# Two mixture-of-experts layers: fewer padded tiles, row copies on another engine, and a longer lead for the staged weights

## The chip, the cores and the metric

One Trainium2 chip, one core of it. The metric is the device time of one execution of the whole program in microseconds, and the number given for a kernel is the median of its timed runs. Lower is better.

## The reference, cut to what matters

The input is 8 sequences of 1024 tokens with 128 features in fp32, 8192 tokens in all. Two layers follow one another, each with an attention part and a mixture-of-experts part, each part added to its input:

```python
x = x + L0_attn(layernorm(x))      # softmax attention, 8 heads of 32, low-rank keys and values
x = x + L0_ffn(layernorm(x))       # 14 experts of width 256, each token goes to its best 2, GELU
x = x + L1_attn(layernorm(x))      # linear attention, 16 heads of 8
x = x + L1_ffn(layernorm(x))       # 8 experts of width 512, each token goes to its best 1, ReLU
```

The second expert part has a limit: an expert keeps at most `ceil(8192 / 8 * 1.25)` = 1280 tokens, those with the highest probability; a token that it turns away goes to expert 0. The first expert part has no limit.

## The kernel before, in words

The program has four stages one after the other: attention of layer 0 (up to about 1335 us), experts of layer 0 (to about 1505), attention and routing of layer 1 (to about 1915), experts of layer 1 (to the end).

**How experts are done.** While routing, the kernel scatters each token's row into a table in HBM (`rows_in` for layer 0, `rows1` for layer 1) that has a region for each expert. The expert stage then walks over tiles of 256 rows (`TW0`), each tile belonging to one expert. How many tiles an expert needs is known only on the chip: its token count over 256, rounded up. `expert_tables` (L147) computes it. `upto` is the running sum of tiles over the experts; `exp_j` (L173) holds the expert of each tile and `row_j` (L188) the first row of each tile. The number of tiles in the program is fixed: `NT0` = 64 + 14 = 78 for layer 0 (L34) and `NT1` = 32 + 8 = 40 for layer 1 (L59). A tile beyond those in use reads a spare region of padding rows; in layer 1 its rows carry a destination that is out of range and are not written.

`looked_up` (L191, load at L198) brings the table entries into registers, six tiles at a time: row numbers to SyncE's registers, expert numbers to VectorE's.

**A tile of layer 0** (L885 to L933), function by function:

- `fetch`: SyncE issues a DMA of 256 rows into `xr` (L888), six buffers.
- `stage`: VectorE copies the weights of the tile's expert from the resident `blob` into `wt` (L896), three buffers. The expert's number comes from a register.
- `turn`: TensorE transposes the rows into `px` (L902), and VectorE copies that from PSUM to `xt` (L904).
- `hidden0`: TensorE multiplies by the first weights into `ph` (L911), and ScalarE applies GELU into `g` (L914).
- `output0`: TensorE multiplies by the second weights into `py` (L921, two buffers), VectorE adds bias (L926) and row (L930) into `y`, and GpSimd issues the DMA to `rows_out` (L931).

The loop (L941 to L956) is software-pipelined and its order is written out by hand for TensorE, VectorE and SyncE (`manual_schedule`, L935). Round j fetches tile j+4, stages and turns tile j+1, does the first product of tile j and the second product of tile j-1. ScalarE and GpSimd are ordered by the scheduler.

**Places.** After the loop in the source, but outside the part with the fixed order, L963 to L970 work out where each token's two results lie in `rows_out`: for each of 8 sequences and 2 choices, four small VectorE operations (compare, multiply, reduce, subtract) give `found`. The scheduler puts these 64 operations early: in the profile they run from 1321.8 to 1347.5 us, among the table computations and the first tiles. The gathers of layer 1 (L1052) read `found`.

**A tile of layer 1** (L1509 to L1564) is the same with a hidden width of 512, so four products into `ph` (L1536), ReLU on ScalarE (L1539), and eight products into `py` (L1546). Its result is scattered straight to the output by two indirect DMAs from GpSimd (L1558). After the 40 tiles every engine loads the number `over`, the largest token count of experts 1 to 7 (L1504), and branches (L1588): if it is over 1280, `dropped` (L1596) finds the tokens that are turned away by bisection and sends them through expert 0, in 16 blocks of 512 tokens.

The order of a round in layer 0's loop, before the change:

```python
if j + 4 < NT0:
    ahead.append(fetch(j + 4))
if ahead:
    t = ahead.pop(0)
    ready.append((t, stage(j + 1), turn(t)))
t, w, xt = ready.pop(0)
made.append((j, t, w, hidden0(w, xt)))
if len(made) > 1:
    output0(*made.pop(0))
```

Of the kernel before, what the change touches and what calls it, by code (L numbers as in the profile page):

```python
# [8 lines left out]
F32 = mybir.dt.float32  # L9
# [19 lines left out]
E0, F0 = 14, 256  # L29
K0 = F0 // P  # L30
CAP0 = NB * T
TW0 = 256
TI0 = TW0 // P
NT0 = 2 * NB * T // TW0 + E0  # L34
REG0 = TW0 + CAP0
ROWS0 = E0 * REG0 + TW0

# [1 line left out]
B_END = B_B2 + D  # L39
# [8 lines left out]
E1, F1 = 8, 512  # L48
# [7 lines left out]
NBLK = NB * T // BLK  # L56


NT1 = NB * T // TW0 + E1  # L59
ROWS1 = E1 * REG0 + TW0  # L60
RW1 = 2 * D + 1
L_W1, L_W2, L_B1, L_B2 = 0, F1, F1 + K1 * D, F1 + K1 * D + K1
# [13 lines left out]
def tile_two_layers(  # L76
# [70 lines left out]
    def expert_tables(tab, psum, ptag, counts, ne, nt):  # L147

        tot = psum.tile([P, ne], F32, name="tot", tag=ptag)
        nc.tensor.matmul(tot, lhsT=ones, rhs=counts, start=True, stop=True)
        per = CAP0 // TW0
        grid = tab.tile([P, ne, per], F32, name="grid")
        nc.vector.tensor_tensor(
            grid, tot.unsqueeze(2).to_broadcast([P, ne, per]),
            cst[:, C_TW:C_TW + per].unsqueeze(1).to_broadcast([P, ne, per]), ALU.is_gt,
        )
        tiles = tab.tile([P, ne], F32, name="tiles")
        nc.vector.tensor_reduce(tiles, grid, AX.X, ALU.add)  # L160
# [27 lines left out]
        nc.vector.tensor_copy(row_j, rj)  # L188
        return SimpleNamespace(exp_j=exp_j, row_j=row_j, base=base, tot=tot)

    def looked_up(table, nt, engine, top):  # L191

# [681 lines left out]
    with ExitStack() as ph:  # L874
# [10 lines left out]
        def fetch(j):  # L885
            r = row_of(j)
            t = work.tile([P, TI0, D], F32, name="xr", bufs=6)
            nc.sync.dma_start(  # L888
                out=t, in_=rows_in[bass.ds(r, TW0), :].rearrange("(p i) d -> p i d", i=TI0)
            )  # L890
            return t

        def stage(j):
            e = expert_of(j)
            t = work.tile([P, 1, B_END], F32, name="wt", bufs=3)
            nc.vector.tensor_copy(t, blob[:, bass.ds(e, 1), :])  # L896
            return t[:, 0, :]

        def turn(t):
            ps = px.tile([P, TI0, P], F32, name="px")  # L900
            for i in range(TI0):
                nc.tensor.transpose(ps[:, i, :], t[:, i, :], ident)  # L902
            xt = work.tile([P, TW0], F32, name="xt", bufs=3)
            nc.vector.tensor_copy(xt, ps.rearrange("p i t -> p (i t)"))  # L904
            return xt

        def hidden0(w, xt):
# [9 lines left out]
        def output0(j, t, w, g):  # L917
# [14 lines left out]
                out=rows_out[j * TW0:(j + 1) * TW0, :].rearrange("(p i) d -> p i d", i=TI0), in_=y  # L932
            )  # L933

        with tc.manual_schedule(  # L935
            engines={mybir.EngineType.PE, mybir.EngineType.DVE, mybir.EngineType.SP}
        ):
            made, ahead = [], [fetch(j) for j in range(4)]
            t = ahead.pop(0)
            ready = [(t, stage(0), turn(t))]  # L940
            for j in range(NT0):  # L941
                if j + 4 < NT0:
                    ahead.append(fetch(j + 4))
                if ahead:
                    t = ahead.pop(0)
                    ready.append((t, stage(j + 1), turn(t)))
                t, w, xt = ready.pop(0)
                made.append((j, t, w, hidden0(w, xt)))
                if len(made) > 1:
                    output0(*made.pop(0))  # L950
                if j == 8:
                    load_layer1()
                    make_layer1()
                if j == NT0 - 8:
                    warm()
            output0(*made.pop(0))  # L956


        shape = [P, CPB, E0]
        for b in range(NB):  # L960
            for k in range(2):
                pick = work.tile(shape, F32, name="pick")
                nc.vector.tensor_tensor(  # L963
                    pick, chosen[:, k, b, :].unsqueeze(2).to_broadcast(shape),
                    cst[:, C_J:C_J + E0].unsqueeze(1).to_broadcast(shape), ALU.is_equal,
                )
                nc.vector.tensor_tensor(pick, pick, tables0.base.unsqueeze(1).to_broadcast(shape), ALU.mult)
                to = work.tile([P, CPB], F32, name="to")
                nc.vector.tensor_reduce(to, pick, AX.X, ALU.add)
                nc.vector.tensor_tensor(found[:, b, k, :], ranks[:, k, b, :], to, ALU.subtract)  # L970

    layer0w.close()


# [518 lines left out]
    with ExitStack() as ph:  # L1493
        tab = ph.enter_context(tc.tile_pool(name="d_tab", bufs=1))
        over = tab.tile([1, 1], mybir.dt.int32, name="over")
        with ExitStack() as main:
            work = main.enter_context(tc.tile_pool(name="d_work", bufs=2))
            px = main.enter_context(tc.tile_pool(name="d_px", bufs=2, space=PSUM))
            ph_ps = main.enter_context(tc.tile_pool(name="d_ph", bufs=4, space=PSUM))
            py_ps = main.enter_context(tc.tile_pool(name="d_py", bufs=2, space=PSUM))  # L1500

            tables = expert_tables(tab, px, "px", counts1, E1, NT1)
            most = tab.tile([1, 1], F32, name="most")
            nc.vector.tensor_reduce(most, tables.tot[0:1, 1:], AX.X, ALU.max)  # L1504
            nc.vector.tensor_copy(over, most)
# [60 lines left out]
            with tc.manual_schedule(  # L1566
                engines={mybir.EngineType.PE, mybir.EngineType.DVE, mybir.EngineType.SP}
            ):
                made, ahead = [], [fetch1(j) for j in range(4)]
                t = ahead.pop(0)  # L1570
                ready = [(t, stage1(0), turn1(t))]
# [12 lines left out]
        crowd = nc.values_load(  # L1584
            over, min_val=0, max_val=NB * T,
            skip_runtime_bounds_check_because="it counts tokens",
        )
# [196 lines left out]
```

## Time and profile before

| What | Value |
|---|---|
| Median of three timed runs | 2098.26 us |
| The three runs | 2098.26, 2090.84, 2103.18 us |
| The profiled execution, its own time | 2095.04 us |
| Its span in the trace | 2093.2 us |
| Mean granted TensorE clock | 0.957 of full speed |
| Busy share of the span: PE, DVE, ACT, POOL | 94%, 69%, 53%, 58% |

The profile is one execution. Its span runs from the first to the last instruction of the program; the 1.8 us between span and time lie around it. PE is TensorE's matmuls, PEld its weight loads, DVE VectorE, ACT ScalarE, POOL GpSimd, SP SyncE. A line number such as L904 is that of the listing above. Times in a timeline or a chain are microseconds from the start of the span. The page's costliest groups belong to layer 0's attention, which takes the first 1300 us. The two expert stages together are about 330 us, so they have to be looked at in windows of their own.

### The profile page before, as it was taken

How to read it: one execution, taken by the hardware profiler on the slowest of the kernel's cores; microseconds unless marked ns; L12 is line 12 of the kernel's file. 1: busy time of each engine (PE TensorE's matmuls, PEld its weight loads, DVE VectorE, ACT ScalarE, POOL GpSimd, SP SyncE). 2: the span in 40 equal slices, each digit the busy share in tenths (PEclk: the TensorE clock that was granted, in tenths of full speed). 3: DMA queues.
4: the chain of work that ended last, by engine and by line, in shares of the span. 5: the costliest groups of instructions: out<-in, count | busy, mean ns of one | idle time of the engine just before them, and what ended most of it. 6: DMA issues, size and time to landing. Idle time of an engine off the chain costs nothing. (4 is left out here: it accounts for less than half of the span.)

```text
span 2093.2 us, 45540 instructions
## 1 busy us (share of the span) xinstructions
PE 1958.7 (94%) x17544; PEld 1015.2 (48%) x17544; DVE 1444.9 (69%) x3762; ACT 1101.3 (53%) x2297; POOL 1212.2 (58%) x1329
## 2 busy tenths in 40 slices
PE   7999999999999999999999997599679999993997
PEld 3333333333333333333333333488657777772996
DVE  6767768758768768768767776777557777763553
ACT  2655555555555555555555453244357666651443
POOL 1556656757667667667667775422364667623555
PEclk9999999999999999999999998699879999986998
DMA  6000000000000000000000000233222211102331
GB/s 223 1 2 2 1 2 3 8 7 9 8 8 8 8 8 9 8 8 8 8 8 13 9 12 29 75 127 127 94 74 81 87 50 51 46 25 81 103 105 49
DMA packets 50896, 82.91 MB, mean 40 GB/s; under 512 B 13849, under 2 KB 32928, under 8 KB 50544
## 3 DMA queue, kind: packets, MB, share of 16 engines
q0 software_dynamic: 18112, 41.69, 6.0%
q1 hardware_dynamic: 29104, 30.29, 5.1%
q10 hardware_dynamic: 3456, 7.95, 1.2%
q8 instruction: 140, 2.29, 0.5%
q14 instruction: 84, 0.69, 0.1%
HBM read 43.92 MB, written 36.61 MB: 38 GB/s over the span
## 5 line engine op out<-in xcount | busy, mean ns | idle before, releaser
L368 DVE TENSOR_REDUCE nmp<-big 128x1 f32<-128x512 f32 x1000 | 642.2, 683 | 295.1 <-PE st L404 257.4
L407 ACT ACTIVATE e<-st 128x512 f32<-128x512 f32 x1000 | 544.3, 595 | 467.7 <-PE st L404 395.6
L238 POOL TENSOR_TENSOR e<-e 128x512 f32<-128x512 f32 x488 | 603.6, 1267 | 50.0 <-PE num L421 50.0
L364 PE MATMUL big<-kT,qT 32*128 32x512 f32 x2000 | 630.5, 641 | 0.2 <-DVE nmp L368 0.2
L404 PE MATMUL st<-qT,kT 32*128 32x512 f32 x2000 | 530.0, 589 | 0.0
L421 PE MATMUL num<-e,v 128*32 128x512 f32 x3064 | 300.7, 465 | 8.5 <-ACT nums L449 8.5
L238 POOL TENSOR_TENSOR outT<-nums,dens 128x64 f32<-128x64 f32 x248 | 79.4, 321 | 376.4 <-DVE dens L439 284.1
L404 PEld LDWEIGHTS st<-qT,kT 32*128 32x128 f32 x2000 | 212.7, 191 | 2.9 <-issue 1.2
L403 PE MATMUL st<-nb,ones_h 3*128 3x512 bf16 x1000 | 210.5, 385 | 1.3 <-DVE nmp L368 1.3
L403 PEld LDWEIGHTS <-ones_h 3*128 3x128 bf16 x1024 | 51.1, 91 | 320.5 <-issue 314.5
L421 PEld LDWEIGHTS num<-e,v 128*32 128x32 f32 x3064 | 61.3, 108 | 296.9 <-issue 264.6
L364 PEld LDWEIGHTS big<-kT,qT 32*128 32x128 f32 x2000 | 194.7, 183 | 21.9 <-DVE nmp L368 17.9
L1052 POOL DMA_INDIRECT got<-rows_out,found x128 | 126.4, 988 | 84.5 <-PE tp L1087 41.8
L606 POOL DMA_INDIRECT rows_in<-xn,at x128 | 131.6, 1028 | 45.0 <-issue 31.5
L439 DVE RECIPROCAL dens<-dens 128x64 f32<-128x64 f32 x248 | 130.0, 537 | 17.1 <-ACT dens L434 17.0
L421 PE MATMUL den<-e,ones 128*32 128x512 f32 x1024 | 141.0, 608 | 0.2 <-POOL e L238 0.2
L1558 POOL DMA_INDIRECT out_x<-y,to x80 | 88.4, 1105 | 81.0 <-DVE y L1556 40.7
L914 ACT ACTIVATE g<-ph,wt 128x256 f32<-128x256 f32 x156 | 70.8, 475 | 115.0 <-PE ph L911 115.0
L1539 ACT ACTIVATE g<-ph,wt 128x256 f32<-128x256 f32 x160 | 70.9, 474 | 100.8 <-PE ph L1536 100.8
L931 POOL DMA_DIRECT2D rows_out<-y x78 | 42.2, 541 | 122.7 <-DVE y L930 118.3
L911 PE MATMUL ph<-xt,wt 128*128 128x256 f32 x312 | 83.3, 390 | 6.2 <-DVE xt L904 6.2
L921 PEld LDWEIGHTS py<-wt,g 128*128 128x128 f32 x624 | 81.9, 192 | 4.1
(283 smaller groups left out, 3003.9 us busy)
## 6 DMA issues: line engine op xcount, KB each, us to landing
xr<-rows SPq DMA_DIRECT2D x40, 257.0 KB
xr<-rows_in SPq DMA_DIRECT2D x78, 128.0 KB
rows_out<-y POOLq DMA_DIRECT2D x78, 128.0 KB, 2.2
nb<-part SPq DMA_DIRECT2D x384, 1.0 KB
blob<-in_blob ACTq DMA_DIRECT2D x8, 578.0 KB
blob<-in_blob SPq DMA_DIRECT2D x1, 4494.0 KB
x<-in_x SPq DMA_DIRECT2D x8, 512.0 KB
rows<-nil ACTq DMA_DIRECT2D x9, 257.0 KB
```

The source lines that it names most:

```text
L238: return tc.keep_in_program_order(f(*args, **kw))
L364: nc.tensor.matmul(ps, lhsT=qTs[n][r, qc * P:(qc + 1) * P], rhs=kTs[n][r, kb * BLK:(kb + 1) * BLK], start=True, stop=True,)
L368: nc.vector.tensor_reduce(nmps[n][:, h, qc, kb:kb + 1], ps, AX.X, ALU.max, negate=True)
L403: nc.tensor.matmul(st, lhsT=ones_h[r3, :], rhs=nbs[n][r3, cols], start=True, stop=False)
L404: nc.tensor.matmul(st, lhsT=kTs[n][r, kc * P:(kc + 1) * P], rhs=qTs[n][r, cols], start=False, stop=True)
L407: nc.scalar.activation(e[:, h, :], st, AF.Exp, scale=SCALE0)
L421: nc.tensor.matmul(vds[key][32 * h:32 * h + 32, cols], lhsT=ones[:, :HD0] if den else vs[b][:, kc, c0:c0 + HD0], rhs=e[:, h, cols], start= ...
L439: nc.vector.reciprocal(s[:, cols], s[:, cols])
L606: ins = nc.gpsimd.indirect_dma_start(out=rows_in, out_offset=bass.IndirectOffsetOnAxis(ap=at[:, k, j:j + 1], axis=0), in_=xn[:, c0 + j, :] ...
L911: nc.tensor.matmul(ps, lhsT=w[:, B_W1 + k * P:B_W1 + (k + 1) * P], rhs=xt, start=True, stop=True)
L1052: ins = tc.keep_in_program_order(nc.gpsimd.indirect_dma_start(out=gots[p][:, i, k, :], out_offset=None, in_=rows_out, in_offset=bass.Indir ...
L1558: ins = nc.gpsimd.indirect_dma_start(out=out_rows, out_offset=bass.IndirectOffsetOnAxis(ap=at[:, i:i + 1], axis=0), in_=y[:, i, :], in_off ...
```

## The change

The change has these parts:

- The tile counts fall by one in each layer: `NT0` = 77 and `NT1` = 39.
- In layer 1 the stage's code becomes a function `tiles1(main, first, last)`. It is called for tiles 0 to 35 (`NT1_MAIN` = 36) ahead of the branch, and for tiles 36 to 38 behind it, before `dropped`. The number `over` becomes the larger of two excesses: of the fullest expert over 1280, and of the tiles in use over 36 (not below 0). The branch is taken if it is above 0.
- The pools of that stage are opened with another setting for waits on memory that is used again (`reuse_waits="tile"`).
- In layer 0, `turn` has ScalarE copy the rows, and ScalarE's order is written out by hand too.
- The weights of layer 0 are staged two tiles ahead in four buffers, and before the turn of a round.
- The places are worked out for four sequences at once: 16 operations on 448 columns, one at the end of each third round from round 16 on.

The constants table loses one column[...]. The instructions of the first attention stage and of the second stand in the same order as before.

The diff, cut to its core:

```diff
-NT0 = 2 * NB * T // TW0 + E0
+NT0 = 2 * NB * T // TW0 + E0 - 1
...
-NT1 = NB * T // TW0 + E1
+NT1 = NB * T // TW0 + E1 - 1
+NT1_MAIN = 36
...
         def stage(j):
             e = expert_of(j)
-            t = work.tile([P, 1, B_END], F32, name="wt", bufs=3)
+            t = work.tile([P, 1, B_END], F32, name="wt", bufs=4)
...
             xt = work.tile([P, TW0], F32, name="xt", bufs=3)
-            nc.vector.tensor_copy(xt, ps.rearrange("p i t -> p (i t)"))
+            nc.scalar.copy(xt, ps.rearrange("p i t -> p (i t)"))
...
+        def places():
+            half = NB // 2 * CPB
+            shape = [P, half, E0]
+            for b in range(0, NB, NB // 2):
+                for k in range(2):
+                    bs = slice(b, b + NB // 2)
+                    pick = work.tile(shape, F32, name="pick", bufs=1)
+                    of_expert = chosen[:, k, bs, :].rearrange("p b c -> p (b c)").unsqueeze(2).to_broadcast(shape)
+                    yield lambda: nc.vector.tensor_tensor(
+                        pick, of_expert, cst[:, C_J:C_J + E0].unsqueeze(1).to_broadcast(shape), ALU.is_equal
+                    )
+                    yield lambda: nc.vector.tensor_tensor(
+                        pick, pick, tables0.base.unsqueeze(1).to_broadcast(shape), ALU.mult
+                    )
+                    to = work.tile([P, half], F32, name="to", bufs=1)
+                    yield lambda: nc.vector.tensor_reduce(to, pick, AX.X, ALU.add)
+                    yield lambda: nc.vector.tensor_tensor(
+                        found[:, bs, k, :], ranks[:, k, bs, :], to.rearrange("p (b c) -> p b c", b=NB // 2),
+                        ALU.subtract,
+                    )
...
         with tc.manual_schedule(
-            engines={mybir.EngineType.PE, mybir.EngineType.DVE, mybir.EngineType.SP}
+            engines={
+                mybir.EngineType.PE, mybir.EngineType.DVE, mybir.EngineType.Activation, mybir.EngineType.SP
+            }
         ):
+            placing = places()
             made, ahead = [], [fetch(j) for j in range(4)]
+            weights = [stage(j) for j in range(2)]
             t = ahead.pop(0)
-            ready = [(t, stage(0), turn(t))]
+            ready = [(t, turn(t))]
             for j in range(NT0):
                 if j + 4 < NT0:
                     ahead.append(fetch(j + 4))
+                if j + 2 < NT0:
+                    weights.append(stage(j + 2))
                 if ahead:
                     t = ahead.pop(0)
-                    ready.append((t, stage(j + 1), turn(t)))
-                t, w, xt = ready.pop(0)
+                    ready.append((t, turn(t)))
+                (t, xt), w = ready.pop(0), weights.pop(0)
                 made.append((j, t, w, hidden0(w, xt)))
...
+                if j >= 16 and j % 3 == 1:
+                    for piece in placing:
+                        piece()
+                        break
             output0(*made.pop(0))
-        shape = [P, CPB, E0]
-        for b in range(NB):
-            for k in range(2):
...
+        def tiles1(main, first, last):
+            work = main.enter_context(tc.tile_pool(name="d_work", bufs=2, reuse_waits="tile"))
...
+            if first == 0:
+                tables.__dict__.update(expert_tables(tab, px, "px", counts1, E1, NT1).__dict__)
+                most = tab.tile([1, 1], F32, name="most")
+                nc.vector.tensor_reduce(most, tables.tot[0:1, 1:], AX.X, ALU.max)
+                more = tab.tile([1, 1], F32, name="more")
+                nc.vector.tensor_scalar(more, tables.upto[0:1, E1 - 1:], float(-NT1_MAIN), 0.0, ALU.add, ALU.max)
+                nc.vector.scalar_tensor_tensor(over, most, float(-CAP1), more, ALU.add, ALU.max)
...
-                for j in range(NT1):
-                    if j + 4 < NT1:
+                for j in range(first, last):
+                    if j + 4 < last:
...
+        with ExitStack() as main:
+            tiles1(main, 0, NT1_MAIN)
...
-        with tc.If(crowd > CAP1):
+        with tc.If(crowd > 0):
+            with ExitStack() as main:
+                tiles1(main, NT1_MAIN, NT1)
             dropped(tc, nc, SimpleNamespace(
```

More of the change, by code (lines that the diff above doesn't have):

```diff
@@ L188, in expert_tables @@
         nc.vector.tensor_copy(row_j, rj)
-        return SimpleNamespace(exp_j=exp_j, row_j=row_j, base=base, tot=tot)
+        return SimpleNamespace(exp_j=exp_j, row_j=row_j, base=base, tot=tot, upto=upto)
     def looked_up(table, nt, engine, top):
@@ L955, in tile_two_layers @@
                     warm()
+                if j >= 16 and j % 3 == 1:
+                    for piece in placing:
+                        piece()
+                        break
             output0(*made.pop(0))
-        shape = [P, CPB, E0]
-        for b in range(NB):
-            for k in range(2):
[L962 to L970, printed above, removed]
+            assert next(placing, None) is None
     layer0w.close()
@@ L1495, in tile_two_layers @@
         over = tab.tile([1, 1], mybir.dt.int32, name="over")
[L1496 to L1505, printed above, removed]
+        tables = SimpleNamespace()
+        def tiles1(main, first, last):
+            work = main.enter_context(tc.tile_pool(name="d_work", bufs=2, reuse_waits="tile"))
+            px = main.enter_context(tc.tile_pool(name="d_px", bufs=2, space=PSUM, reuse_waits="tile"))
+            ph_ps = main.enter_context(tc.tile_pool(name="d_ph", bufs=4, space=PSUM, reuse_waits="tile"))
+            py_ps = main.enter_context(tc.tile_pool(name="d_py", bufs=2, space=PSUM, reuse_waits="tile"))
+            if first == 0:
[5 more added lines that the diff above has]
+                nc.vector.scalar_tensor_tensor(over, most, float(-CAP1), more, ALU.add, ALU.max)
             row_of1 = looked_up(tables.row_j, NT1, mybir.EngineType.SP, E1 * REG0)
@@ L1568, in tile_two_layers @@
             ):
-                made, ahead = [], [fetch1(j) for j in range(4)]
+                made, ahead = [], [fetch1(j) for j in range(first, min(first + 4, last))]
                 t = ahead.pop(0)
-                ready = [(t, stage1(0), turn1(t))]
-                for j in range(NT1):
-                    if j + 4 < NT1:
+                ready = [(t, stage1(first), turn1(t))]
+                for j in range(first, last):
+                    if j + 4 < last:
                         ahead.append(fetch1(j + 4))
@@ L1582, in tile_two_layers @@
                 output1(*made.pop(0))
+        with ExitStack() as main:
+            tiles1(main, 0, NT1_MAIN)
         crowd = nc.values_load(
             over, min_val=0, max_val=NB * T,
-            skip_runtime_bounds_check_because="it counts tokens",
+            skip_runtime_bounds_check_because="it is made of counts",
         )
-        with tc.If(crowd > CAP1):
+        with tc.If(crowd > 0):
+            with ExitStack() as main:
+                tiles1(main, NT1_MAIN, NT1)
             dropped(tc, nc, SimpleNamespace(
```

## The prediction

> **What bounds the kernel now.** I read the 40 slices first (PE is at 9 nearly throughout), then the sums of the two expert stages by window, then the chain of waits, and last the waits and the timeline inside layer 0's expert stage. The columns of the window view are the stretch, its length, busy time of PE, PEld, DVE, ACT and POOL with instruction counts, granted clock, DMA share, GB/s:
>
> ```profile
> 1335.00:1503.00 168.00, 160.08 (x1092) 147.96 (x1092) 127.84 (x341) 70.80 (x156) 47.73 (x92) 0.98 0.37 123
> ...
> 1928.00:2078.00 150.00, 149.79 (x1031) 141.14 (x1032) 75.42 (x195) 70.90 (x160) 84.39 (x76) 0.99 0.33 94
> ```
>
> Layer 1's stage (second line) is PE alone: 149.79 of 150.00 us. Layer 0's leaves 8 us of PE idle, so it stalls. The chain gives the price of a layer-1 tile:
>
> ```profile
> 2062.50 0.22 PE px L1527 x2
> 2062.72 1.73 PE ph L1536 x8
> 2064.45 1.78 PE py L1546 x16
> 2066.24 0.22 PE px L1527 x2
> ```
>
> From px to px is 2066.24 - 2062.50 = 3.74 us (3.73 in nearly all tiles), all PE. Layer 0's tile has half of the ph and py work: 0.22 + 1.73/2 + 1.78/2 = 1.975 us, which is what its timeline shows where it runs smoothly. Where it doesn't:
>
> ```profile
> 1398.94 0.42 DVE L930 TENSOR_TENSOR y<-y,xr 128x256 f32<-128x256 f32 x1
> ...
> 1400.56 0.50 DVE L896 COPY wt<-blob 128x642 f32 x1 [1.19 <-ACT g L914]
> 1400.97 0.42 DVE L904 COPY xt<-px 128x256 f32<-128x256 f32 x1
> ...
> 1401.44 1.13 PE L911 MATMUL ph<-xt,wt 128*128 128x256 f32 x4 [0.80 <-DVE xt L904]
> ```
>
> VectorE finishes an output at 1399.36 and starts nothing until 1400.56. The named releaser, ACT's g, is two tiles old and long done; what sits there is the register load of the next six expert numbers (L198). Behind it on the same queue stand the weight copy and then the copy of the turned rows, and PE waits for the latter. The waits of the stretch 1333 to 1504 count it, once for each six tiles:
>
> ```profile
> DVE wt L896 <- ACT g L914: 10.6, 12, 1.2
> PEld ph L911 <- DVE xt L904: 9.0, 12, 1.0
> ```
>
> ```profile
> L198 DVEq TENSOR_LOAD <-exp_j x20: 361/944/1417, 1327.5 to 2059.3; - x20
> ```
>
> From the starts of ph in the timeline, a stalled group has intervals 2.94 + 2.08 or 2.37 + 2.08 in place of 2 x 1.975: 1.07 or 0.50 us lost, six of each, 9.4 us. First to last ph is 162.3 us; 77 x 1.975 is 152.1; the other us is the first two intervals (2.13, 2.83), where PE's matmuls still run at a lower clock.
>
> [...] the 1.19 us gap holds two ready copies. [...] the same copy in layer 1 (L1088) has 372 to 398 and 347 to 373 ns in its two groups. [...] L914's load took 1283[...].
>
> **The change, part by part.** (a) *Layer 1, 40 tiles to 36 ahead of the branch*: 4 x 3.73 = 14.9 us off the path. All else that a tile issues (one SP fetch, three VectorE copies, two adds, four ScalarE activations, two POOL scatters) lies beside PE and goes too. It holds only if the branch isn't taken: at most 36 tiles in use and no expert beyond 0 with over 1280 tokens. The reference's router, counted on the given inputs, has 922 965 913 1187 1267 982 1082 874 tokens: 4+4+4+5+5+4+5+4 = 35 tiles, largest 1267. The trace says the same: a full tile writes 128 KB per 3.73 us, 35 GB/s, but the stretch in which tiles 36 to 38 are scattered moves
>
> ```profile
> 2066.40:2077.50 11.10, 11.10 (x80) 10.48 (x79) 4.91 (x14) 5.31 (x12) 6.43 (x6) 1.00 0.03 8
> ```
>
> 8 GB/s, so those tiles are empty; and no line of `dropped` runs. The tail after the last matmul (2077.2 to 2093.2) keeps its steps. Before the stage the test for the branch has one more tiny VectorE operation: the like of it (L1505) is 0.06 us in the chain, +0.1.
>
> (b) *Layer 0, 78 tiles to 77*: 1.97 us, the one fewer tile being an empty one (the counts make 72).
>
> (c) *The stall at register loads*: the turned rows leave VectorE, so no load stands ahead of them; weights are two tiles ahead, so ph(j+1) has had its weights for a tile. What is late next is the bias add y. VectorE's work per tile falls to wt 0.49 + y 0.42 + y 0.42 = 1.33 of 1.97. A load of 1.2 us makes one y start about 0.85 + 1.2 + 0.49 - 1.97 = 0.6 us late. PE needs that py buffer (two of them) only 2 x 1.97 - 1.05 = 2.9 us after the matmuls that filled it; 0.6 + 0.42 is within it. So all 9.4 us go. If the cover failed, they stay.
>
> (d) *Row copies on ScalarE*: 77 x 0.37 = 28 us of ACT work, from L1088. Per tile ACT has 0.91 (the pair of Gelus) + 0.37 = 1.28 of 1.97. What queues behind the copy's wait for px(j+1) is the Gelu pair of tile j, but PE runs px(j+1) ahead of ph(j), so that wait ends first; who waits for Gelu is py(j), one round later. The copy has a whole round until ph(j+1). Cost 0; uncovered it could be 0.37 per tile, 28 us. PE's ph and first py wait on two semaphores now. In layer 1 ph does that already, its extra 51 ns wait running ahead while PE is busy: 0.
>
> (e) *Table load*: the program order puts the Gelu table behind the first two row copies, where it lay idle-side at 1313.78 before. The second copy would end at about 1337.7, Gelu start at 1339.0 instead of 1338.1 and end near 1340.0; PE first wants g at 1340.85. Hidden by 0.9 us[...]. I take +0.3, bounds 0 and +1.3.
>
> (f) *Start*: two weight copies (0.5 each) now stand before the row table on VectorE, and the small place operations that stood among the tables are gone: table about 0.5 us later than 1330.1. SP then loads it (0.8 to 1.0 us) but fetches only when the last scatter of rows (1331.10, landing 2.3 us later) is in:
>
> ```profile
> 1329.91 0.18 DVE L188 CAST row_j<-rj 1x78 int32<-1x78 f32 x1
> ...
> 1331.10 0.95 POOL L606 DMA_INDIRECT rows_in<-xn,at  x1 [0.30 <-DMA rows_in<-xn,at]
> ...
> 1333.53 15.69 SPq L888 DMA_DIRECT2D xr<-rows_in  x10
> ```
>
> Slack about 1.7 us, so 0. Fetches per tile and what SP passes are else unchanged.
>
> (g) *Places in 16 grouped operations*, one per third tile from 16 to 61: 448-wide, like L155's grid and L160's reduction (0.62 and 0.61), in all 4 x (0.62 + 0.62 + 0.61 + 0.2) = 8.2 us of VectorE. 1.33 + 0.62 = 1.95 just fits a tile; with a load beside it y is some 1.2 us late, still within 2.9. They issue no DMA; their first reader is the gather at 1508.9, 30 us after the last. Their early time (1321.8 to 1347.5) frees nothing on the path: start is set by the scatter (f), then by PE's clock. Bounds -1.0 and 0; I take 0.
>
> (h) Not part of the edit, but movable: the last rows_out issue stands 2.93 us with no releaser shown. It may go: -2.9 to 0; I take 0.
>
> Sum: -14.9 + 0.1 - 2.0 - 9.4 + 0.3 = -25.9. The profiled execution took 2095.04 (span 2093.2), giving 2069.1. The three timed runs have 2090.84, 2098.26, 2103.18; from their median it is 2072.4. The mean of all four is 2096.8; from it I forecast 2071.
>
> **Rivals.** *Stalls stay* (c fails: the load's lateness reaches PE through the py buffers): 2071 + 9.4 = 2080. For it: VectorE has only 0.64 us spare per tile. Against: 2.9 us of room. Chance 0.09. *ScalarE's order binds* (d fails: PE waits about 0.24 us, the wait seen after px at L904's late copies, in each of 77 tiles): +18, 2089. Against: a round of slack. Chance 0.06. *More is gained* ((h) and (g) at their ends): 2071 - 3.9 = 2067. Chance 0.11. *The branch is taken*, the one that ends slower: 3 tiles of 3.73 plus `dropped`, whose 16 blocks of 512 tokens cost PE two tiles' worth each: 16 x 7.46 = 119, together 130 us, about 2201. It decides from 37 tiles or from 1281 tokens in one expert; margins are two tiles and 13 tokens, and only rounding on the chip could move them. Chance 0.02.
>
> **Numbers.** Forecast 2071, chance 0.72, own spread about 2064 to 2077 from the runs' scatter. The range 2060 to 2084 takes in the stalls and the further gain with that scatter, and leaves out the last two rivals. About 0.5%, 10.5 us, is what a measurement of this kernel can tell from no change; only a saving under that (above 2087.8) is the middle: faster 0.94, same 0.04, slower 0.02.
>
> **What would show it.** In the new profile: 36 layer-1 tiles at 3.73; layer 0's ph intervals 1.97 at register loads too, PE near 150 busy of 152; no PE wait on xt; VectorE's gaps still there but with y late. Wrong if ph waits for ACT's xt, if py waits for y, or if lines of `dropped` run.

## The result and the profile after

The changed kernel takes 2073.82 us in the median of four runs (2071.68 to 2076.24). The kernel before, with one more run beside those shown, takes 2096.18 (2090.84 to 2103.18). The ratio is 0.9885 with a 95% interval of 0.9858 to 0.9911. The forecast was 2071, in a range of 2060 to 2084.

The profiled execution of the changed kernel took 2075.58 us, with a span of 2073.8 and a mean granted clock of 0.952. The profiled execution before took 2095.04, with 2093.2 and 0.957. Cut at the same events, the two spans compare like this (us):

| Stretch | before | after | difference |
|---|---|---|---|
| start to the first hidden product (ph) of layer 0 | 1337.01 | 1337.33 | +0.32 |
| first to last tile of layer 0, by the start of ph | 162.32 | 150.70 | -11.62 |
| last tile's ph to the first gather of layer 1 | 9.58 | 10.06 | +0.48 |
| first gather to the tables of layer 1's tiles (attention and routing) | 406.89 | 414.21 | **+7.32** |
| tables to the first layer-1 tile | 10.64 | 10.59 | -0.05 |
| first transpose to last ph of layer 1 | 148.61 | 133.40 | -15.21 |
| to the end | 18.11 | 17.49 | -0.62 |
| sum | 2093.2 | 2073.8 | -19.4 |

So the two expert stages gave what they should, and more than a quarter of it went again in a stage whose order of instructions no edit touches. First the parts that hold. The sums by window of the changed kernel (same columns as before) have layer 0's experts and a stretch of layer 1's:

```profile
1335.50:1491.50 156.00, 154.66 (x1078) 145.62 (x1078) 102.17 (x246) 99.07 (x232) 48.92 (x91) 0.98 0.40 131
1924.50:2060.00 135.50, 135.50 (x933) 127.46 (x932) 68.07 (x176) 63.84 (x144) 75.64 (x69) 0.99 0.32 94
```

PE is idle for 1.3 of 156 us in layer 0, where it was idle for 8 of 168. VectorE's share fell and ScalarE's rose. The chain of work through layer 1 shows the same tile as before, now 36 times:

```profile
2040.02 0.22 PE px L1554 x2
2040.24 1.73 PE ph L1563 x8
2041.97 1.78 PE py L1573 x16
2043.76 0.22 PE px L1554 x2
```

2043.76 - 2040.02 = 3.74 us. The register load in layer 0 looks like this in the timeline (it runs on VectorE's queue from 1393.91 to 1395.33):

```profile
1393.46 1.03 PE L913 MATMUL ph<-xt,wt 128*128 128x256 f32 x4
1393.90 0.42 DVE L932 TENSOR_TENSOR y<-y,xr 128x256 f32<-128x256 f32 x1
...
1395.43 1.03 PE L913 MATMUL ph<-xt,wt 128*128 128x256 f32 x4
1395.52 0.50 DVE L898 COPY wt<-blob 128x642 f32 x1 [1.20 <-ACT g L916]
1395.93 0.42 DVE L928 TENSOR_TENSOR y<-py,wt 128x256 f32<-128x256 f32 x1
...
1397.41 1.03 PE L913 MATMUL ph<-xt,wt 128*128 128x256 f32 x4
```

VectorE's hole of 1.20 us is still there, as forecast, and the bias add behind it is late (2.49 us after the one before, not 1.97). PE's products start at 1393.46, 1395.43 and 1397.41 all the same: the hole reaches no one. In the waits of the stretch 1333 to 1492 (engine and line, what it waited for, us in total, times, longest) the hole is the same twelve as before, and PE waits for nothing but the first rows:

```profile
ACT xt L906 <- PE px L904: 75.1, 76, 23.0
...
PE px L904 <- DMA xr<-rows_in: 17.0, 2, 16.8
...
DVE wt L898 <- ACT g L916: 10.6, 12, 1.3
```

### The profile page after: what moved, and what is told of

Same layout as the page of the kernel before. It is cut to its first block, busy times and chain, and to the rows that moved or that the text cites. A ratio compares the mean times of both kernels' runs of the same rounds, so it can differ in the third digit from the quotient of the medians.

```text
span 2073.8 us, 45378 instructions
## 1 busy us (share of the span) xinstructions
PE 1947.8 (94%) x17426; PEld 1005.2 (48%) x17426; DVE 1407.3 (68%) x3614; ACT 1121.2 (54%) x2356; POOL 1204.4 (58%) x1320
## 5 line engine op out<-in xcount | busy, mean ns | idle before, releaser
L366 PEld LDWEIGHTS big<-kT,qT 32*128 32x128 f32 x2000 | 194.6, 183 | 21.9 <-DVE nmp L370 17.9
L1585 POOL DMA_INDIRECT out_x<-y,to x72 | 79.3, 1102 | 74.7 <-DVE y L1583 58.0
L1566 ACT ACTIVATE g<-ph,wt 128x256 f32<-128x256 f32 x144 | 63.8, 474 | 92.6 <-PE ph L1563 92.6
L1037 POOL TENSOR_TENSOR rs<-ve,mhalf 128x2 f32<-128x2 f32 x64 | 46.4, 726 | 62.0 <-DVE ve L1035 53.5
L923 PE MATMUL py<-wt,g 128*128 128x128 f32 x616 | 81.0, 275 | 0.0
```

The costliest lines, as they stand in the source:

```text
L366: nc.tensor.matmul(ps, lhsT=qTs[n][r, qc * P:(qc + 1) * P], rhs=kTs[n][r, kb * BLK:(kb + 1) * BLK], start=True, stop=True,)
L923: nc.tensor.matmul(ps[:, i, :], lhsT=g[:, k, i * P:(i + 1) * P], rhs=w[:, B_W2 + k * D:B_W2 + (k + 1) * D], start=k == 0, stop=k == K0 - 1,)
L1585: ins = nc.gpsimd.indirect_dma_start(out=out_rows, out_offset=bass.IndirectOffsetOnAxis(ap=at[:, i:i + 1], axis=0), in_=y[:, i, :], in_off ...
```

## Where the 7 us went: reading the attention stage

The windows of the stage from the first gather on, first its first 62 us and then the whole of it, in the kernel before:

```profile
1508.90:1570.90 62.00, 41.15 (x525) 27.45 (x526) 33.48 (x119) 31.89 (x82) 42.98 (x46) 0.76 0.28 74
1508.91:1915.80 406.89, 363.36 (x5334) 262.39 (x5334) 272.52 (x1069) 240.40 (x618) 236.62 (x256) 0.89 0.21 61
```

and in the changed kernel:

```profile
1498.10:1560.10 62.00, 42.91 (x378) 27.15 (x383) 26.75 (x94) 25.50 (x65) 36.19 (x39) 0.56 0.25 65
1498.10:1912.31 414.21, 372.54 (x5334) 268.77 (x5334) 272.79 (x1068) 240.44 (x618) 236.17 (x256) 0.87 0.20 60
```

The work is the same: 5334 products, and equal busy time on VectorE, ScalarE and GpSimd. Only PE, with its weight loads, is longer, by 9 us of busy time. In its first 62 us it gets through 378 products where it did 525, because the granted clock is 0.56 in place of 0.76. The clock's record has two values in both profiles, 1.0 (full) and 0.5 (half). Before, PE is at half clock from 1504.7 for 30.7 us; after, from 1494.4 for 58.0 us. In the whole stage it is at half clock for 89.4 us before and 110.4 after. 7.3 us more stage for 21 us more of half clock is 0.35 us per us.

**The theory tested** is that this is a draw of the clock that differs from one execution to the next and has nothing to do with the edits. **The rival** is that an edit causes it (the grouped places or the earlier gathers shift the stage), so that the kernel's real gain is about 19 us. A third possibility is that the two profiles come from different chips, since which chip they ran on is not on record; "The size", further below, comes back to it.

## The experiments

The runs came in four sets, each on one chip beside the kernel before: the first four of the table, the next four, the next three, and the last. The sets ran on four different chips, so lengths of a stage are compared within a set. Since the clock differs between executions, the times are also compared at equal half-clock time. For each run the half-clock time is 2 x (1 - mean granted clock) x span; the mean clock has three decimals, which leaves about 2 us of it open. A least-squares fit over the runs of a set has one slope for all and one level for each kernel. The slopes are 0.345, 0.388, 0.343 and 0.382 us per us (standard errors 0.016 to 0.020), and the residual is 1.4 to 1.8 us. The last column is the difference of the levels, with its standard error.

| Kernel | median, us | before beside it | ratio, 95% interval | layer 0 loop, us | at equal half clock |
|---|---|---|---|---|---|
| after_again | 2086.36 | 2119.73 | 0.9843, 0.9806 to 0.9880 | 149.96 | -27.9 +- 0.8 |
| l0_only | 2105.39 | 2119.73 | 0.9929, 0.9896 to 0.9963 | 151.55 | -13.9 +- 0.7 |
| l1_only | 2096.30 | 2119.73 | 0.9898, 0.9861 to 0.9934 | 162.15 | -16.4 +- 0.8 |
| warm_gap | 2084.11 | 2119.73 | 0.9840, 0.9801 to 0.9879 | 150.70 | -22.2 +- 1.0 |
| undo_copy | 2090.17 | 2118.76 | 0.9881, 0.9803 to 0.9960 | 161.77 | -15.1 +- 1.2 |
| undo_lead | 2083.65 | 2118.76 | 0.9817, 0.9768 to 0.9866 | 156.89 | -21.3 +- 1.2 |
| undo_places | 2085.59 | 2118.76 | 0.9827, 0.9774 to 0.9879 | 151.31 | -27.4 +- 1.2 |
| warm_stage | 2091.84 | 2118.76 | 0.9868, 0.9818 to 0.9918 | 151.55 | -11.8 +- 1.4 |
| shift24 | 2070.40 | 2099.01 | 0.9860, 0.9823 to 0.9896 | 150.02 | -26.6 +- 0.7 |
| shift8 | 2068.77 | 2099.01 | 0.9861, 0.9827 to 0.9896 | 151.52 | -27.3 +- 0.7 |
| undo_reuse | 2074.88 | 2099.01 | 0.9883, 0.9848 to 0.9918 | 151.51 | -26.6 +- 0.7 |
| tile77 | 2126.99 | 2124.70 | 1.0002, 0.9973 to 1.0030 | 160.98 | -1.4 +- 0.6 |

The loop is first to last tile by the start of ph in one profile; before has 162.32.

### after_again: the changed kernel once more

No edit. It ran beside the next three.

> The changed kernel once more, as the control of this group. In the first profile all steps gave what was forecast except the attention stage of layer 1, which no edit touches: from its first gather to the start of the tables it took 414.2 us in place of 406.9. Clock theory: TensorE's granted clock stayed at half for 58 us after layer 0's experts in place of 31, and how long it stays is not set by the edits, so this run's stage time will follow its own half-clock time (about 405 to 415 us, whatever it is). Edit theory: an edit costs the stage 7 us, so it is 414 again, whatever the clock does. Both: ratio 0.986 to 0.991.

Measured: ratio 0.9843, a little below the range that was expected. At equal half-clock time it is 27.9 us faster; the forecast's sum is 25.9. In its profile the attention stage lasts 431.12 us, outside what either theory had expected. It has 110.3 us of half clock, as the changed kernel's first profile had (110.4 us in a stage of 414.21). With the same kernel and the same half-clock time, neither an edit nor the time at half clock explains these 17 us. All four profiles of this set have a long stage (421 to 431 us) and all three of the third set a short one (407 to 412), so the chip is the likely cause. This run alone could not separate the theories.

### l0_only and l1_only: the two halves of the change

`l0_only` has layer 1 as before; `l1_only` has layer 0 as before. Against the changed kernel:

```diff
-NT1 = NB * T // TW0 + E1 - 1
-NT1_MAIN = 36
+NT1 = NB * T // TW0 + E1
...
```

```diff
-NT0 = 2 * NB * T // TW0 + E0 - 1
+NT0 = 2 * NB * T // TW0 + E0
...
-            nc.scalar.copy(xt, ps.rearrange("p i t -> p (i t)"))
+            nc.vector.tensor_copy(xt, ps.rearrange("p i t -> p (i t)"))
...
```

> Layer 0's edits alone (77 tiles, row copies on ScalarE, weights two ahead, grouped places); layer 1's experts as before with 40 tiles. By the forecast the first gather is 11 us earlier than before. Clock theory: the total is 2096 - 11 = 2085 plus or minus what the clock does in the attention stage (up to 8 either way). Edit theory with layer 0's edits as the cause: the stage takes 414, the total is 2092.

> Layer 1's edits alone (36 tiles ahead of the branch); layer 0 as before with 78 tiles. By the forecast 4 tiles of 3.73 us: 2096 - 14.9 = 2081, ratio 0.993, with layer 0's stage and the attention stage as before. Clock theory: the attention stage may differ from 406.9 by its half-clock time. Edit theory with layer 1's edits as the cause: the stage takes 414, total 2088.

Measured: -13.9 and -16.4 at equal half-clock time, where the forecast's steps give -11.1 and -14.8. Together that is -30.3, where both at once give -27.9. The difference is 2.4 +- 1.2 us, so the halves add up only within two standard errors. Layer 0's half gains 2.8 us more than forecast, which its profile does not show: the loop is 10.8 us shorter than before and the step to the first gather 0.5 us longer. The cause of this is open, and the last column should be trusted to 2 or 3 us rather than to its standard errors. The attention stage had 111.6 us of half clock in `l0_only` and 83.3 in `l1_only`. That looked like a tie to layer 0's edits. It did not last: see `undo_places`, `shift24` and the half-clock times of the timed runs below.

### warm_gap and warm_stage: more work for PE in the gap

Products that nothing reads, put where PE waits for the gathers; `warm_stage` has both pieces, `warm_gap` the first.

```diff
             output0(*made.pop(0))
+            hot = px.tile([P, TI0, P], F32, name="px")
+            for i in range(36):
+                nc.tensor.matmul(
+                    hot.rearrange("p i t -> p (i t)"), lhsT=ident, rhs=cst[:, :TW0], start=True, stop=True
+                )
...
+        hot1 = pk.tile([P, H1 * VW], F32, name="sums")
+        for i in range(36):
+            nc.tensor.matmul(hot1, lhsT=ident, rhs=cst[:, :H1 * VW], start=True, stop=True)
```

> The changed kernel plus 36 matmuls that nobody reads (128x256, about 15.6 us at full clock) on TensorE between layer 0's last tile and layer 1's attention, where it is idle for 18 us. They put nothing on the path. Clock theory: the clock is full up to about 1510 us, the half-clock stretch after that is shorter than 58 us, and the stage goes from 414 towards 405: 3 to 9 us faster than the changed kernel, some 2067. Edit theory: no difference, 2074.

> The changed kernel with 36 unread matmuls of 128x256 after the last tile of layer 0, and 36 of 128x144 more after the first projection of layer 1's attention, which only add work to TensorE. Clock theory (the attention stage of layer 1 lasts about 0.33 us longer for each us at half clock): half-clock time in that stage falls from about 110 us to 80 us or less, the stage shortens by about 10 us, and the added work gives back 3 to 6 us of it; at equal half-clock time it is slower than the changed kernel by 3 to 8 us. Rival, the stage's 7.3 us are a cost of the edits (places of the data, order of the queues): the stage stays as long as in the changed kernel whatever the clock does.

Measured: the windows of the stage in `after_again` and, on the same chip, in `warm_gap` are these:

```profile
1500.45:1931.57 431.12, 377.94 (x5334) 271.02 (x5334) 272.11 (x1069) 239.19 (x618) 236.68 (x256) 0.87 0.19 57
1496.51:1918.33 421.82, 380.24 (x5373) 272.56 (x5371) 271.69 (x1069) 239.48 (x618) 236.37 (x256) 0.91 0.20 59
```

Half-clock time in the stage falls from 110.3 to 77.5 us, and the stage is 9.3 us shorter with all edits of the change in place, which the rival rules out. `warm_stage` adds nothing to that: its stage has 50.1 us of half clock, where `undo_places` on the same chip has 88.8, but it lasts 419.32 us to 419.92. The second piece and the end of the first are work inside the stage, and PE is busy there for 11.7 us more. In the timed runs the half-clock time of the whole span is 165.9 us on average in `warm_gap` to 189.2 in `after_again`, and 159.9 in `warm_stage` to 182.2 in `undo_places`.

But the work put in is dear: at equal half-clock time `warm_gap` is 5.7 us slower than `after_again`, and `warm_stage` 15.6 us slower than `undo_places` beside it. The 3 to 9 us that `warm_gap` was expected to gain did not come (2.3 us by the medians), and the 3 to 8 us of cost expected of `warm_stage` were too low. Neither beats the changed kernel by more than the intervals.

### undo_copy and undo_lead: which part took the stall away

```diff
-            nc.scalar.copy(xt, ps.rearrange("p i t -> p (i t)"))
+            nc.vector.tensor_copy(xt, ps.rearrange("p i t -> p (i t)"))
```

> The changed kernel with one part undone: the row copies of layer 0 are back on VectorE (weights still two tiles ahead, places in groups). Stall theory with the copy at fault: the register load sits in VectorE's queue ahead of a row copy that TensorE needs within the same tile, so about 6 waits of 1.0 us and 6 of 0.5 us come back, and the grouped places, which now share VectorE with the copies, add a few more; layer 0's loop is 9 to 15 us longer than the 150.6 us of the changed kernel, nothing else moves. Rival, the lead of the weights at fault: the loop stays within 2 us of 150.6. Times are to be compared at equal half-clock time (0.345 us per us), since TensorE's clock differs from run to run.

Measured: a loop of 161.77 us, 11 more than the changed kernel, and 12.3 +- 1.3 us slower than `undo_places` beside it at equal half-clock time. All twelve stalls are back, and rounds with a place operation cost 0.08 to 0.2 us besides. The timeline of `undo_copy`, VectorE and PE behind a register load:

```profile
1396.84 0.50 DVE L898 COPY wt<-blob 128x642 f32 x1 [1.18 <-ACT g L916]
1397.25 0.42 DVE L906 COPY xt<-px 128x256 f32<-128x256 f32 x1
...
1397.72 1.13 PE L913 MATMUL ph<-xt,wt 128*128 128x256 f32 x4 [0.79 <-DVE xt L906]
```

The weight copy here is for a tile further on and nobody needs it yet, but the row copy stands behind it in the queue and PE needs that at once. The lead of the weights alone is worth nothing: the stalled intervals are as long as before (2.93 and 2.38 us), and `tile77` below, with neither lead nor move, has a loop of 160.98.

```diff
-            t = work.tile([P, 1, B_END], F32, name="wt", bufs=4)
+            t = work.tile([P, 1, B_END], F32, name="wt", bufs=3)
...
-            weights = [stage(j) for j in range(2)]
+            weights = [stage(0)]
...
-                if j + 2 < NT0:
-                    weights.append(stage(j + 2))
+                if j + 1 < NT0:
+                    weights.append(stage(j + 1))
```

> The changed kernel with one part undone: weights one tile ahead (three buffers), row copies still on ScalarE. Copy theory: the weight copy has a whole tile of 1.97 us before TensorE needs it and the register load takes about 1 us of that, so the loop is 0 to 3 us longer than 150.6 us. Rival, the lead is what removed the stalls: 9 us or more come back, as waits of TensorE on the weight copy.

Measured: 156.89 us, 6.2 and 6.9 more than in the two profiles of the changed kernel; that lies between the two theories and within neither. The timeline of `undo_lead` at a load:

```profile
1379.96 0.37 ACT L906 COPY xt<-px 128x256 f32<-128x256 f32 x1 [0.69 <-PE px L904]
...
1381.82 0.50 DVE L898 COPY wt<-blob 128x642 f32 x1 [0.71 <-ACT g L916]
1381.94 0.37 ACT L906 COPY xt<-px 128x256 f32<-128x256 f32 x1 [0.69 <-PE px L904]
...
1382.46 1.10 PE L913 MATMUL ph<-xt,wt 128*128 128x256 f32 x4 [0.62 <-DVE wt L898]
```

The rows of this product were copied at 1379.96, a round earlier; the row copy at 1381.94 is that of the next tile. VectorE's weight copy, behind the load, ends at 1382.32, and PE now waits for the weights. (The waits view gives five of the six such waits, 2.8 of 3.4 us, to ScalarE's row copy. In those five the row copy ends about 0.05 us after the weight copy; PE starts 0.14 to 0.15 us after the weight copy in all six.)

The loads on VectorE's queue come in two lengths in turn, about 1.42 and 0.82 us. The long one makes a tile 0.7 to 0.8 us longer, six times, the short one 0.17, five times, and the tile after each is 0.07 longer. The copy's move and the lead are therefore not two gains. PE waits for the last copy that it needs behind the load. Before the change that is the row copy, and the lead alone does not touch it. With the row copy moved alone it is the weight copy, which ends earlier: a load then costs about 0.8 or 0.24 us, where it cost 1.07 or 0.50. Only both together free PE.

### undo_places and undo_reuse: the parts priced at nothing

`undo_places` brings back the 64 small operations in place of the 16 grouped ones. `undo_reuse` opens layer 1's pools as before:

```diff
-            work = main.enter_context(tc.tile_pool(name="d_work", bufs=2, reuse_waits="tile"))
+            work = main.enter_context(tc.tile_pool(name="d_work", bufs=2))
...
```

> The changed kernel with one part undone: the 64 small place operations as before, not 16 in groups between the tiles. Forecast's price of this part 0: the loop and the step from the last hidden matmul to the first gather are unchanged within 0.5 us. Rival: the small operations take VectorE's slack and 1 to 3 us come back in the loop, or between the loop and the first gather.

> The changed kernel with one part undone: the pools of layer 1's tiles wait for their buffers as before, not tile by tile. Forecast's price of this part 0: layer 1's tiles stay at 3.73 us and the span at equal half-clock time within 1 us. Rival: the part is worth the 1 to 2 us by which layer 1 gained more at equal half-clock time than the 14.8 us of the forecast.

Measured: -27.4 and -26.6 at equal half-clock time, where the changed kernel has -27.9 in `after_again`, and -26.6 and -27.3 with the memsets of `shift24` and `shift8`: neither part can be told from 0. The loops are 151.31 and 151.51, 0.6 and 0.8 us longer than in the changed kernel's first profile. Their second interval at PE's lower clock is longer (3.08 and 3.45 us for 2.64), and the rest is 1.975 us.

`undo_places` has all edits of layer 0 but the grouped places, and its attention stage has 88.8 us of half clock, about as in the kernel before (89.4) and in `l1_only` (83.3). That speaks against the rival for all those edits; `shift24` below has the places too.

### shift24, shift8 and tile77: GpSimd's pause

Before, the last `rows_out` stood 2.93 us with no releaser shown, step (h) of the forecast. GpSimd's timeline, before and after:

```profile
1505.94 0.54 POOL L931 DMA_DIRECT2D rows_out<-y  x1 [2.93 <-issue]
1508.91 0.99 POOL L1052 DMA_INDIRECT got<-rows_out,found  x1 [2.43 <-issue]
```

```profile
1492.07 0.54 POOL L933 DMA_DIRECT2D rows_out<-y  x1 [0.35 <-DVE y L932]
1498.10 0.99 POOL L1072 DMA_INDIRECT got<-rows_out,found  x1 [5.50 <-issue]
```

The pause is gone from one instruction and is in front of the next: 2.93 + 2.43 = 5.36 us before, 0.35 + 5.50 = 5.85 after. Its last wait in the record ends at 1494.80, so 3.3 us have no cause shown.

```diff
+        for _ in range(24):
+            nc.gpsimd.memset(restart1[:, :, 0], 0.0)
```

> The changed kernel with 24 more small memsets on GpSimd's queue early in layer 0 (they set again what is set already). In the kernel before, GpSimd pauses 2.9 us before the last rows_out although VectorE is done; in the changed kernel it doesn't, and pauses 3.3 us before the first gather instead, with no wait left open. Theory of place: the pause belongs to a place in GpSimd's list of instructions, as if the next instructions were not there yet; 24 instructions more in front move it by that many instructions, so it falls among the tiles of layer 0, where GpSimd has time, and the step from the last hidden matmul to the first gather shrinks from 10.1 to about 7 us. Rival, a hidden wait (the gather needs something that the trace does not show, such as the landing of the last rows_out): the pause stays, 10.1 us.

> The same with 8 memsets. Theory of place: 8 places are less than the 11 instructions between the last rows_out but one and the first gather, so the pause moves to just before or just after the last rows_out, or stays if the pause sits at larger steps; the step from the last hidden matmul to the first gather is between 7 and 10.1 us. Rival, a hidden wait of the gather: 10.1 us, as with 24.

Measured: 10.07 us from the last tile to the gather in both, as in the changed kernel, and the pause still in front of the gather (`shift24`):

```profile
1509.90 1.00 POOL L1074 DMA_INDIRECT got<-rows_out,found  x1 [5.50 <-issue]
```

The theory of place falls. The next run has one edit of the change alone, on the kernel before:

```diff
-NT0 = 2 * NB * T // TW0 + E0
+NT0 = 2 * NB * T // TW0 + E0 - 1
```

> The kernel before with one edit alone: 77 tiles in layer 0. Forecast's price: one tile of 1.97 us less, all twelve stalls still there: loop 160.3 to 161 us from first to last hidden matmul, where before has 162.3, and 2.0 us less at equal half-clock time. For GpSimd's pause: if it goes with the number of tiles (with the number of waits on its queue), it moves from the last rows_out to the first gather, as in the changed kernel, and the step from the last hidden matmul to the gather is 9.4 us in place of 8.9; if it goes with the other edits of layer 0, the pause stays at the last rows_out and the step at 8.9 us.

Measured: a loop of 160.98 us, the stalls all there, and -1.4 +- 0.6 us at equal half-clock time. The step is 10.07 us (9.4 in its expectation, which counts from the tile's last hidden matmul), with the pause in front of the gather:

```profile
1505.25 1.00 POOL L1052 DMA_INDIRECT got<-rows_out,found  x1 [5.50 <-issue]
```

So the pause goes with the number of tiles. In `l1_only`, with 78 tiles, the step is 9.58. What GpSimd does in these 3 us is not settled; a wait of the gather that the trace doesn't show fits all of these profiles, but it was not shown.

`shift24` gave the clearest answer to the other question. It has every edit of the change, and the clock happened to fall as in the kernel before: at half clock for the first 30.7 us, 89.8 us in the stage. Its windows:

```profile
1509.90:1571.90 62.00, 41.26 (x526) 27.57 (x527) 33.48 (x119) 31.96 (x82) 42.49 (x46) 0.76 0.26 75
1509.90:1917.16 407.26, 363.70 (x5334) 263.15 (x5334) 272.75 (x1069) 240.27 (x618) 235.96 (x256) 0.89 0.19 61
```

407.26 us and 363.70 busy, where before has 406.89 and 363.36. With the clock alike, the stage is alike, to 0.4 us. On the same chip `undo_reuse` has 97.3 us of half clock and 407.94, and `shift8` 104.5 and 411.68.

And the edits do not draw more half clock. Over the timed runs of the first, second and third set, before has 197.7, 202.2 and 189.1 us of it in the whole span on average. The changed kernel (`after_again`) has 189.2 beside the first, `undo_places` 182.2 beside the second, and `shift24`, `shift8` and `undo_reuse` 186.3, 187.6 and 192.6 beside the third.

## Why the prediction was right, step by step

- **(a) Layer 1, 14.9 us.** Right: the stage is 15.2 us shorter at the same 3.73 us a tile, the branch is not taken, and the test for it cost nothing visible (10.64 to 10.59). `l1_only` has 16.4 +- 0.8 at equal half-clock time. The forecast left the end of the program as it was. It got 0.6 us shorter: it lasts 17.9 to 18.1 us in the profiles with 40 tiles, and 17.0 to 17.5 in those with 36, apart from 18.6 in `warm_gap`. `undo_reuse` shows no gain from the pools' setting. The rest of the excess is within two errors.
- **(b) and (c) Layer 0, 2.0 + 9.4 us.** Right in sum: 11.6 us. All twelve stalls are gone, and the intervals are 1.975 except the first two. One tile alone has 1.3 in the loop (`tile77`), 0.6 less than its term; its first three intervals are together 0.6 us longer than those of before, the third with a wait of 0.82 us for a row copy. The reason given named both the move of the row copies and the lead of the weights, but not what each is worth. Without the first, 11 us come back; without the second, about 6. The lower tile counts remain enough for any routing: 16384 rows for 14 experts need at most 64 + 13 tiles of 256, and 8192 rows for 8 experts at most 32 + 7.
- **The late bias add.** Right: forecast 0.6 us late, measured 2.49 - 1.97 = 0.5, and no wait of PE on py.
- **(d) Row copies on ScalarE, 0.** Right: 77 copies of 372 to 374 ns, and the only wait of theirs is that for px.
- **(e) Table load, +0.3.** The order was right and the cost is not seen. ScalarE's timeline:

```profile
1337.58 0.37 ACT L906 COPY xt<-px 128x256 f32<-128x256 f32 x1 [0.50 <-PE px L904]
1337.97 1.28 ACT L916 ACT_TABLE_LOAD   x1
1339.26 0.84 ACT L916 ACTIVATE g<-ph,wt 128x256 f32<-128x256 f32 x2
```

  The load stands behind two copies and takes 1.28 us. The first GELU starts as it ends, 1.2 us later than before (1339.26 for 1338.11). Both the term of 0.3 and its bound of 1.3 were the author's estimates. PE's first interval is 2.13 us in both kernels. The 0.32 us at the start arose earlier: the last scatter of rows is 0.4 us later too. That they equal the term is chance.
- **(f), (g) Start and places, 0.** Right for the places (`undo_places`). The start is the 0.32 us later; `undo_reuse`, with the same order up to there, has its first hidden product at 1336.67 in place of 1337.33, so that much can be the execution.
- **(h) The pause, 0.** Right in sum and not in kind: the pause did not stay where it was. It moved, and cost 0.5 us.
- **The size.** The steps sum to -25.9. The profiles differ by -19.4, because the stage between them cost 7.3 us more. The sum compared two executions as if PE's clock were the same. The spread given to the forecast (2064 to 2077) was taken from the runs' scatter, without saying that this scatter is the clock's. At equal half-clock time the complete change measures -27.9 +- 0.8 (`after_again`). With a part undone, or memsets added, that makes no measurable difference, it measures -26.6 to -27.4 on the chips of the second and the third set. The first two profiles can be brought to equal half-clock time too, as an estimate: their mean clocks give 180.0 and 199.1 us at half clock, and with the third set's slope of 0.343 the difference of -19.5 between the two times becomes -26.0. Their levels, 2033.3 and 2007.3 us, lie within 1 us of those of the third set, so two different chips are not what separates them. So the steps were right to about 2 us. The distance of 2.8 us between 2071 and the median 2073.8 is of the size of the scatter; that it is no larger is partly luck, since single runs of `after_again` lie 14 us apart.

In the clock's record of the first two profiles the stretches at half clock that fall in this stage last 3.41, 6.83, 13.65, 30.72, 40.96 and 58.03 us, whole multiples of the shortest. A busy PE was not enough for full clock here: from 1521 to 1552 us of the changed kernel PE is busy for 30.60 of 31.00 us, at a granted clock of 0.50. Why the same list of instructions leaves half clock 27 us after its first gather in one execution and 54 us after it in another isn't settled.

Of the versions run, none beats the changed kernel by more than its measurement can tell. `shift8`, `shift24` and `undo_places` are the same as it at equal half-clock time.

## What to carry to other kernels

A queue that stalls in front of several ready instructions must be cleared of all of them that the next engine needs soon: here the row copy and the weight copy were late together, and either edit alone gave only part (a loop of 156.89 us) or nothing (161.77), where neither left 160.98 and both gave 150.70. When two profiles differ in a stage with the same instructions and the same busy time on all engines but PE, compare the granted clock in windows (here 0.56 against 0.76 in the first 62 us) before looking for a cause in the edit, and compare timed runs on one chip and at equal half-clock time. A few us of gain are then seen that medians alone hide.

## What the runs showed of the hardware

- An execution of the kernel before or after, without matmuls added, has 163 to 248 us at half clock, and each us of it costs 0.34 to 0.39 us of time. That accounts for nearly all scatter between the runs of a kernel on one chip: what is left is 1.4 to 1.8 us.
- At equal half-clock time, chips still differ. The kernel before has a level of 2050.4 in the first set and 2033.6 in the third, 17 us apart. In the attention stage of layer 1, `l1_only`'s profile on the first set's chip has 421.25 us at 83.3 us of half clock, where `shift24`'s on the third set's has 407.26 at 89.8. Brought to the same half-clock time, an estimate with slopes of 0.345 and 0.343, that is 16 us, so most of the distance between these two chips lies in this stage. The cause was not looked for.
- In layer 0's loop the register loads on VectorE's queue take about 1.42 and 0.82 us, mostly in turn, and VectorE starts nothing else meanwhile (1.20 us idle in the timeline above, 10.6 us over the twelve loads). The twelve loads of the kernel before take 0.81 to 1.42 us, those of the changed kernel 0.61 (the last one) to 1.55, and those of `undo_lead` 0.61 to 1.47.
- With matmuls added that nothing reads there was less half clock: in the stage 77 us in place of 110 with 36 of them, and on another chip 50 in place of 89 with 72; in the timed runs' whole span, 165.9 in place of 189.2 and 159.9 in place of 182.2. With 36 of them the median stayed within the intervals, 2084.11 against 2086.36; with 72 it was 2091.84 against `undo_places`' 2085.59.
